# Turning the scan's sums once per block in four row groups, with the last products by C one unit earlier

## The chip, the cores and the metric

The kernel runs on one core of a Trainium2 chip. The metric is the device time of one execution in microseconds, from the first instruction to the last. A core has a matrix engine, TensorE (PE, with its weight loads listed as PEld), and three vector engines: VectorE (DVE), ScalarE (ACT) and GpSimd (POOL). SyncE (SP) issues the DMAs. Each engine works through its own queue in order, and a semaphore makes an instruction wait for one of another engine. Matmul results go to PSUM, which has eight banks of 512 fp32 columns on 128 partitions.

## What is computed

Two layers are applied to 16 images of 256 channels by 1024 tokens, each with a residual. The first is a transformer block. The second, which sets the order of the whole kernel, is a selective scan over the tokens, for 512 channels with 64 states each:

```
x = x + attention_and_mlp(group_norm(x))          # 4 heads of 32, LayerNorm, GELU
xs = group_norm(x) + pos
u, z = split(xs @ in_proj_w.T);  u = silu(causal_conv4(u))
dt, Bm, Cm = split(u @ x_proj_w.T)
delta = softplus(dt @ dt_proj_w.T + dt_proj_b);  A = -exp(A_log)
def step(h, (d_t, B_t, C_t, u_t)):                # h: 512 channels x 64 states
    h = exp(d_t[..., None] * A) * h + (d_t * u_t)[..., None] * B_t[:, None, :]
    y = einsum('bdn,bn->bd', h, C_t)
y = (ys + u * D) * silu(z);  x = x + (y @ out_proj_w.T) * sigmoid(conv3(xs))
```

The change concerns `y`: the sum over the 64 states of h times C, for each channel and each token.

## The kernel before, in words

**Units and blocks.** A unit is two channels: 2 x 64 states fill the 128 partitions, and 1024 tokens lie along the row. An image has 256 units. Eight units with slots i = 0 to 7 make a block of 16 channels, so an image has 32 blocks and the run has 4096 units in 512 blocks. The parity of a block is `e`. It says which of the two buffers `h0` and `h1` (128 x 8 x 1024) its scans fill.

**One unit** takes five instructions or so. `load` (L900) brings delta times u of its two channels from memory as `dub`, spread over the states (512 KB). `inputs` (L905) multiplies this by B on GpSimd. `decay` (L914) has two bf16 matmuls spread delta into the two banks of a tile `a`, and an exponential on ScalarE (L916) turns it into the decay. There are two `a` tiles, so the decay of unit n + 2 can start when the scan of unit n has read its tile. `scan` (L922) runs the recurrence on VectorE, 1024 steps in one instruction, into slot i of the block's buffer. `dub` has seven buffers; loads run six units ahead and multiplies four.

**The output of a block** (`outputs`, L939 to L979) is made while the next block is scanned. It has three stages, all in the one PSUM bank `yb`:
- *Products by C* (L955). The 1024 tokens are taken in 128 pieces of eight. For each piece a matmul with 32 columns of `cd`, which holds C on a diagonal, as weights and `h` at those eight tokens (64 columns of eight slots by eight tokens) as moving data writes 32 partitions. Each is an fp32 matmul, of which the profile shows two instructions. Two matmuls accumulate (c = 0, 1), and four in a row (g = 0 to 3) write the four groups of 32 partitions. Sixteen such sets of eight matmuls are numbered by r and s.
- *Copy* (L962). After the four sets of one r, ScalarE copies columns 0 to 255 of the bank to a tile `y2`. There are four copies per block.
- *Turns* (L945). Eight matmuls per r, with every eighth column of `y2` as weights and a constant `turn` as moving data (16 columns), put channels and tokens in an order in which they can be written to memory. They write 32 partitions, the same ones for all eight of an r, in columns 256 to 511. After the fourth r, ScalarE copies the result (64 x 256) to `yo` (L969), and eight DMAs (L977) of 8 KB each write it to `ys`.

**The order.** `outputs` is a generator. It hands control back at each `yield`, and the main loop takes one step of it per unit. In the loop a unit issues the load of unit n + 6, the multiply of n + 4, the scan of n, the decay of n + 2, then one or more steps of side work, and then one step of the running outputs. On each engine the program order is kept as it is recorded. A new block's `outputs` starts at its successor's slot 0, after the running one has had its step. The first eight steps have two sets of products each; the copy of r follows at the end of its second step, and its turns stand in the third step from its start, behind the next products. The fourth turn and the copy to `yo` are the ninth step, at slot 0 of the block after, and the DMAs are the twelfth.

Two waits follow from the buffers. The first scan of a block overwrites the `h` buffer of the block two before it, whose last products are the eighth step of that block's `outputs`, issued one unit earlier. And the first products of a block write the bank from which `yo` has just been copied.

**Side work** are the steps of attention and projections of the next image and of the gated output of the previous image. `rate_for` spreads them by their listed shares over the 256 units of an image. In the last image only the gated output of the one before is left.

The functions and lines that the steps below speak of:

Of the kernel before, what the change touches and what calls it, by code (L numbers as in the profile page):

```python
# [11 lines left out]
F32 = mybir.dt.float32  # L12
# [7 lines left out]
P = 128  # L20
# [30 lines left out]
def attention_then_scan_kernel(  # L51
# [18 lines left out]
    nc = tc.nc  # L70
    B = x.shape[0]

    def pool(name, bufs, **kw):
        return ctx.enter_context(tc.tile_pool(name=name, bufs=bufs, **kw))
# [8 lines left out]
    blk = pool("blk", 2)  # L83
    hst = pool("hst", 1)
# [77 lines left out]
    for k in range(ND):  # L162
# [4 lines left out]
        for j in range(2):  # L167
# [3 lines left out]
                start=(j == 0), stop=(j == 1),  # L171
# [3 lines left out]
    for e in range(2):  # L175
        some = ident[ds(64 * e, 48), ds(64 * e, 48)].rearrange("p (r j i) -> p r i j", r=3, j=2)
# [11 lines left out]
    turn = const.tile([P, 8, 2, 8], F32, name="turn")  # L188
# [27 lines left out]
    yb = yps.tile([P, HL], F32, name="yb", tag="yb")  # L216
# [721 lines left out]

    def outputs(b, k, q, e):  # L939
        hbuf = now["h", e]  # L940

        def turned(r, y2):
            some = yb[ds(32 * (r // 2), 32), 256:].rearrange("p (j a m x) -> p a x j m", j=2, a=2, m=8)
            for x in range(8):
                nc.tensor.matmul(  # L945
                    some[:, r % 2, x], y2[:, x : 256 : 8], turn[:, x], start=True, stop=True
                )

        y2 = None
        for r in range(4):  # L950
            for s in range(4):
                for c in range(2):
                    for g in range(4):
                        at = 256 * s + 64 * r + 16 * g + 8 * c
                        nc.tensor.matmul(  # L955
                            yb[ts(g, 32), ts(s, 64)],
                            cd[:, at // 16, ts(c, 32)], hbuf[:, :, at : at + 8],
                            start=(c == 0), stop=(c == 1),
                        )
                if s == 3:  # L960
                    y2 = blk.tile([P, 256], F32, name="y2", tag="y2")
                    nc.scalar.copy(y2, yb[:, :256])  # L962
                if s == 1 and r > 0:
                    turned(r - 1, y2)
                if s % 2 == 1:
                    yield
        turned(3, y2)
        yo = blk.tile([P, 256], F32, name="yo", tag="yo")
        nc.scalar.copy(yo[:64], yb[:64, 256:])  # L969
        for _ in range(3):  # L970
            yield
        to = state[b]["ys"][ds(k * P + 32 * q, 32)].rearrange(
            "(j i e) (s h c) -> e h s i j c", j=2, e=2, s=4, h=2
        )
        for h in range(2):
            for s in range(4):
                nc.sync.dma_start(  # L977
                    to[e, h, s], yo[ds(32 * h + 8 * s, 8)].rearrange("p (j c) -> p j c", j=2)
                )  # L979

    def prepare(b):
        return chain(first_norm(b), attention_layer(b), scan_inputs(b))
# [26 lines left out]
    for n, (b, k, q, e, i) in enumerate(units):  # L1009
        at = n % UNITS  # L1010
# [32 lines left out]
        if i == 0 and n > 0:  # L1043
            g = outputs(*units[n - 1][:4])
            next(g)
            running.append(g)
# [3 lines left out]
    for _ in outputs(*units[-1][:4]):  # L1050
        pass
# [71 lines left out]
```

## Time and profile before

| | |
|---|---|
| median of three runs | 15706.54 us (15690.69 to 15712.8) |
| the profiled execution, whole | 15708.14 us |
| its span, first to last instruction | 15706.0 us |
| mean granted TensorE clock | 0.725 of full speed |
| scans (L922), DVE | 4096, mean 2279 ns, 9238.5 us busy |
| multiplies (L905), POOL | 4096, mean 2391 ns, 9745.2 us busy |
| decay exponentials (L916), ACT | 4096, mean 1090 ns, 4464.5 us busy |
| copies to y2 (L962), ACT | 2048, mean 373 ns, 764.7 us busy |
| copies to yo (L969), ACT | 512, mean 365 ns, 187.0 us busy |

A row of groups gives the busy time of all instructions of one line and kind, the mean of one, and then the idle time of the engine just before them with what ended most of it. A row of waits names who waited for whom, the total, how often and the longest. In the timeline, equal neighbours are merged, and the brackets give the idle time ahead and its releaser. The view by windows gives for each stretch the busy time of each engine, the granted TensorE clock (1.00 is full), the share of DMA time, and GB/s. Busy time of PE is the union of its matmuls, of which several can run at once.

### The profile page before, as it was taken

The numbers are of one execution on the slowest core, as the hardware profiler recorded it, in microseconds if no ns is written. First come the engines' busy times: TensorE is split into PE (matmuls) and PEld (weight loads), VectorE is DVE, ScalarE is ACT, GpSimd is POOL, SyncE is SP. The second block draws the span as 40 slices with busy tenths as digits, with TensorE's granted clock in tenths as the row PEclk, the third lists the DMA queues.
The fourth block names the chain that finished last, engine by engine and source line by source line (L and its number), as shares of the span: only waits on it lengthen the run. The fifth ranks groups of instructions, "written<-read, shape, count | busy, mean of one in ns | idle before, by whom it ended". The sixth has DMA issues, their size and how long they took to land. (4 is left out here: it accounts for less than half of the span.)

```text
span 15706.0 us, 430046 instructions
## 1 busy us (share of the span) xinstructions
PE 12119.9 (77%) x186800; PEld 7304.2 (47%) x186800; DVE 11806.3 (75%) x7560; ACT 7635.3 (49%) x10421; POOL 9749.9 (62%) x4105
## 2 busy tenths in 40 slices
PE   7677877878778687787878878788787877878777
PEld 2344444444444444444444444444444444444455
DVE  3777787777877878778777787877877778677887
ACT  2455454545545545444554445545455454544544
POOL 0566666666666666566666666666666666666687
PEclk8776777767677676776767767677676877767756
DMA  1456455564555645556455565655556455564566
GB/s 53 168 172 206 159 185 188 174 204 158 190 177 173 205 161 192 174 174 203 162 191 181 171 200 166 197 172 176 196 172 203 163 181 195 167 206 161 183 220 203
DMA packets 989294, 2820.54 MB, mean 180 GB/s; under 512 B 175682, under 2 KB 319299, under 8 KB 987396
## 3 DMA queue, kind: packets, MB, share of 16 engines
q1 hardware_dynamic: 987396, 2793.03, 53.8%
q8 instruction: 1460, 23.92, 0.6%
q14 instruction: 438, 3.59, 0.1%
HBM read 2513.82 MB, written 261.62 MB: 177 GB/s over the span
## 5 line engine op out<-in xcount | busy, mean ns | idle before, releaser
L905 POOL TENSOR_TENSOR dub<-dub,bt 128x1024 f32<-128x1024 f32 x4096 | 9745.2, 2391 | 5895.1 <-DMA dub<-dus 5445.8
L922 DVE TENSOR_TENSOR_SCAN h<-a,dub 128x1024 f32<-128x1024 f32 x4096 | 9238.5, 2279 | 3031.0 <-ACT a L916 1458.8
L916 ACT ACTIVATE a<-a,acol 128x1024 f32<-128x1024 f32 x4096 | 4464.5, 1090 | 5315.2 <-PE a L914 5266.9
L914 PE MATMUL a<-pieces,pick 48*128 48x512 bf16 x8192 | 2054.2, 494 | 2669.0 <-DVE h L922 2578.7
L955 PEld LDWEIGHTS yb<-h,cd 128*32 128x32 f32 x131072 | 2713.8, 138 | 2812.5 <-issue 1522.2
L955 PE MATMUL yb<-h,cd 128*32 128x64 f32 x131072 | 3530.5, 266 | 549.1 <-ACT yo L969 334.2
L945 PEld LDWEIGHTS yb<-turn,y 128*32 128x32 f32 x32768 | 2222.6, 158 | 479.8 <-issue 269.5
L945 PE MATMUL yb<-turn,y 128*32 128x16 f32 x32768 | 2317.3, 216 | 32.5 <-ACT y L962 31.4
L914 PEld LDWEIGHTS <-pick 48*128 48x128 bf16 x8192 | 551.7, 96 | 3032.9 <-issue 2683.2
L962 ACT COPY y<-yb 128x256 f32<-128x256 f32 x2048 | 764.7, 373 | 1229.2 <-PE yb L955 1213.0
L435 PE MATMUL s_ps<-k,q 32*64 32x512 f32 x4092 | 851.6, 724 | 45.1 <-DVE mx L416 39.7
L491 PE MATMUL av<-pt,vv 128*64 128x512 f32 x2048 | 757.6, 828 | 2.2 <-ACT sums L480 1.6
L416 DVE TENSOR_REDUCE mx<-s_ps 128x1 f32<-128x512 f32 x1023 | 647.2, 676 | 110.6 <-PE s_ps L435 110.6
L503 PE MATMUL st_ps<-sp 33*128 33x512 f32 x2048 | 727.2, 794 | 2.9 <-ACT pt L511 2.9
L511 ACT ACTIVATE pt<-st_ps 128x512 f32<-128x512 f32 x1024 | 554.0, 595 | 186.7 <-PE st_ps L503 185.6
L688 PE MATMUL g_ps<-w,xp 128*128 128x256 f32 x1464 | 511.3, 495 | 0.0
L688 PEld LDWEIGHTS g_ps<-w,xp 128*128 128x128 f32 x1464 | 386.4, 327 | 89.9 <-issue 67.4
L969 ACT COPY yo<-yb 64x256 f32<-64x256 f32 x512 | 187.0, 365 | 481.6 <-PE yb L945 398.4
L674 DVE SCALAR_TENSOR_TENSOR u<-up,cwh,u 128x1024 f32<-128x1024 f32 x192 | 351.5, 1831 | 37.1 <-ACT u L666 36.9
L491 PEld LDWEIGHTS av<-pt,vv 128*64 128x64 f32 x2048 | 124.6, 165 | 512.2 <-issue 501.9
L435 PEld LDWEIGHTS s_ps<-k,q 32*64 32x64 f32 x4092 | 193.5, 148 | 343.0 <-DVE mx L416 248.1
L859 PE MATMUL m_ps<-w,xs 128*128 128x256 f32 x1024 | 335.9, 481 | 13.9 <-DVE xs L834 13.9
(177 smaller groups left out, 7029.1 us busy)
## 6 DMA issues: line engine op xcount, KB each, us to landing
dub<-dus SPq DMA_DIRECT2D x4096, 512.0 KB
ys<-yo SPq DMA_DIRECT2D x4096, 8.0 KB
dps<-pc SPq DMA_DIRECT2D x384, 128.0 KB
pieces<-dps SPq DMA_DIRECT2D x1024, 48.0 KB
xs<-in_x_dram SPq DMA_DIRECT2D x64, 512.0 KB
xs<-kept SPq DMA_DIRECT2D x64, 512.0 KB
zs<-z SPq DMA_DIRECT2D x64, 512.0 KB
ud<-u SPq DMA_DIRECT2D x64, 512.0 KB
```

The source lines that it names most:

```text
L416: nc.vector.tensor_reduce(mx[:, g, c, hf : hf + 1], s, AX.X, ALU.max)
L435: nc.tensor.matmul(waiting[g][0][ts(e, 64)], q4[r, ts(c, 64)], k4[r, hs(hf)], start=True, stop=True,)
L491: nc.tensor.matmul(av[ts(e, 2 * DH)], vv[j // (NJ // 2)][:, j % (NJ // 2), 2 * pair + e, :], pts[e], start=(j == 0), stop=(j == NJ - 1),)
L503: nc.tensor.matmul(s, ka[r, ts(j, P)], qa[r, hs(hf)], start=True, stop=True)
L688: nc.tensor.matmul(ps[:, ts(q, C)], xp[k][:, ds(first + t, P, 4)], wg_s[:, k, t, :], start=(k == 0 and t == 0), stop=False,)
L905: nc.gpsimd.tensor_tensor(v, v, blocks[units[n][0]]["bt"], ALU.mult)
L914: nc.tensor.matmul(a[:, hs(hf)], w, pieces[r], start=True, stop=True)
L916: nc.scalar.activation(a, a, AF.Exp, scale=acol[:, at : at + 1])
L922: nc.vector.tensor_tensor_scan(now["h", e][:, i, :], decays.pop(n), loaded.pop(n), 0.0, ALU.mult, ALU.add)
L945: nc.tensor.matmul(some[:, r % 2, x], y2[:, x : 256 : 8], turn[:, x], start=True, stop=True)
L955: nc.tensor.matmul(yb[ts(g, 32), ts(s, 64)], cd[:, at // 16, ts(c, 32)], hbuf[:, :, at : at + 8], start=(c == 0), stop=(c == 1),)
L962: nc.scalar.copy(y2, yb[:, :256])
```

## The change

The sums of a block are kept in one tile `y2` of 128 x 4 x 256, and all 32 turns are made in one step, after all products. For each of the eight x, four turns in a row write the four groups of 32 partitions. The pieces of eight tokens are dealt out by r and s the other way round. The products of one r go to one half of the bank, those of the next to the other half (`(r + e) % 2`), and the turns go to the first 128 columns of half `e`. The yields move: the seven steps with products have 3, 2, 2, 2, 2, 2 and 3 sets, the eighth step has the turns, the ninth the copy to `yo` (128 x 128 now), and the twelfth two DMAs of 32 KB in pieces of 64 tokens (256 bytes), where there were eight DMAs with pieces of 128 tokens.

```
     def outputs(b, k, q, e):
         hbuf = now["h", e]
-        def turned(r, y2):
-            some = yb[ds(32 * (r // 2), 32), 256:].rearrange("p (j a m x) -> p a x j m", j=2, a=2, m=8)
-            for x in range(8):
-                nc.tensor.matmul(
-                    some[:, r % 2, x], y2[:, x : 256 : 8], turn[:, x], start=True, stop=True
-                )
-        y2 = None
+        y2 = hst.tile([P, 4, 256], F32, name="y2", tag="y2")
         for r in range(4):
             for s in range(4):
                 for c in range(2):
                     for g in range(4):
-                        at = 256 * s + 64 * r + 16 * g + 8 * c
+                        at = 256 * r + 64 * s + 16 * g + 8 * c
                         nc.tensor.matmul(
-                            yb[ts(g, 32), ts(s, 64)],
+                            yb[ts(g, 32), ds(256 * ((r + e) % 2) + 64 * s, 64)],
...
-                if s == 3:
-                    y2 = blk.tile([P, 256], F32, name="y2", tag="y2")
-                    nc.scalar.copy(y2, yb[:, :256])
-                if s == 1 and r > 0:
-                    turned(r - 1, y2)
-                if s % 2 == 1:
+                if (r, s) in ((0, 2), (1, 0), (1, 2), (2, 0), (2, 2), (3, 0)):
                     yield
-        turned(3, y2)
-        yo = blk.tile([P, 256], F32, name="yo", tag="yo")
-        nc.scalar.copy(yo[:64], yb[:64, 256:])
+            nc.scalar.copy(y2[:, r], yb[:, ts((r + e) % 2, 256)])
+        yield
+        some = yb[:, ds(256 * e, P)].rearrange("p (j m x) -> p x j m", j=2, m=8)
+        for x in range(8):
+            for r in range(4):
+                nc.tensor.matmul(
+                    some[ts(r, 32), x], y2[:, r, x:256:8], turn[:, x], start=True, stop=True
+                )
+        yield
+        yo = blk.tile([P, P], F32, name="yo", tag="yo")
+        nc.scalar.copy(yo, yb[:, ds(256 * e, P)])
         for _ in range(3):
             yield
         to = state[b]["ys"][ds(k * P + 32 * q, 32)].rearrange(
-            "(j i e) (s h c) -> e h s i j c", j=2, e=2, s=4, h=2
+            "(j i e) (a c) -> e j a i c", j=2, e=2, a=16
         )
-        for h in range(2):
-            for s in range(4):
-                nc.sync.dma_start(
-                    to[e, h, s], yo[ds(32 * h + 8 * s, 8)].rearrange("p (j c) -> p j c", j=2)
-                )
+        for j in range(2):
+            nc.sync.dma_start(to[e, j], yo[:, ts(j, 64)])
```

The number of matmuls of each kind and their shapes stay: 128 products and 32 turns per block.

## The prediction, on record before the changed kernel was run

> **What bounds the kernel now.** I read the page's first part and its groups, then the list of waits, then the scan rows of the whole trace, then single blocks in the timeline, and last the busy times by stage.
>
> ```profile
> PE 12119.9 (77%) x186800; PEld 7304.2 (47%) x186800; DVE 11806.3 (75%) x7560; ACT 7635.3 (49%) x10421; POOL 9749.9 (62%) x4105
> ...
> L955 PE MATMUL yb<-h,cd 128*32 128x64 f32 x131072 | 3530.5, 266 | 549.1 <-ACT yo L969 334.2
> ...
> L945 PE MATMUL yb<-turn,y 128*32 128x16 f32 x32768 | 2317.3, 216 | 32.5 <-ACT y L962 31.4
> ```
>
> No engine is full; two are near it. A quarter as many instructions keep TensorE (PE) busy for two thirds as long in the turns (L945) as in the products by C (L955). Sixteen turn rows in one column group take 1.13 us (mean of 2047 bursts), 32 product rows over four groups 0.86 us (0.65 at full clock).
>
> ```profile
> DVE h L922 <- ACT a L916: 1458.8, 838, 8.4
> DVE h L922 <- PE yb L955: 1058.5, 310, 8.2
> ```
> ```profile
> PE a L914 <- DVE h L922: 2578.7, 1488, 11.3
> PE yb L955 <- ACT yo L969: 334.2, 511, 5.3
> PE yb L955 <- ACT y L962: 193.9, 320, 3.4
> ```
>
> These are VectorE's (DVE) and PE's waits (total, times, longest). Scans wait for products, and decay matmuls (L914) wait for scans: the two engines stop each other in turn. From the starts of the 4096 scans: in the second to fifteenth image, a block's eight scan-to-scan gaps are 2.82, 2.89, 4.72, 3.46, 3.78, 3.26, 3.11 and 6.24 us, of which DVE is busy 2.8 to 3.15. So the gap into the next block idles 3.41 us and the third gap 1.57, of some 7.2 per block. The timeline shows one boundary:
>
> ```profile
> 8597.54 0.65 PE L955 MATMUL yb<-h,cd 128*32 128x64 f32 x32
> 8601.05 0.61 PE L914 MATMUL a<-pieces,pick 48*128 48x512 bf16 x2 [2.86 <-DVE h L922]
> 8601.43 1.94 PE L503 MATMUL st_ps<-sp 33*128 33x512 f32 x4
> 8603.30 1.97 PE L491 MATMUL av<-pt,vv 128*64 128x512 f32 x4
> 8605.20 1.17 PE L945 MATMUL yb<-turn,y 128*32 128x16 f32 x16
> 8606.83 1.08 PE L955 MATMUL yb<-h,cd 128*32 128x64 f32 x32 [0.45 <-ACT yo L969]
> ```
> ```profile
> 8598.71 6.65 DVE L922 TENSOR_TENSOR_SCAN h<-a,dub 128x1024 f32<-128x1024 f32 x3 [3.96 <-PE yb L955]
> 8609.69 2.29 DVE L922 TENSOR_TENSOR_SCAN h<-a,dub 128x1024 f32<-128x1024 f32 x1 [4.32 <-ACT a L916]
> ```
>
> The old block's last products end at 8598.2. Only then may the first scan overwrite that buffer, after 3.96 us of DVE idleness, and only after this scan does the next decay run, after 2.86 us of PE idleness. Three scans pass; the fourth waits 4.32 us, because PE first did side work, turn, wait for yo, and products. PE's clock suffers too (us busy per engine, then granted clock):
>
> ```profile
> 8593.03:8596.44 3.41, 3.41 (x79) 1.72 (x79) 1.72 (x1) 2.64 (x5) 2.35 (x1) 1.00 0.69 190
> 8596.44:8599.86 3.42, 1.75 (x48) 1.43 (x48) 1.15 (x1) 1.39 (x2) 2.37 (x2) 1.00 0.40 151
> 8599.86:8603.27 3.41, 2.22 (x6) 0.67 (x5) 3.41 (x3) 1.09 (x1) 2.34 (x1) 0.50 0.16 64
> ```
>
> After a window with PE busy 1.75 of 3.42 us, the next is at half clock. Hence L503 takes 1.94 us there and 1.02 at full clock.
>
> The stages differ. Two of them, from the same view (scores; attention values):
>
> ```profile
> 8386.30:8478.20 91.90, 78.66 (x1200) 38.35 (x1199) 81.61 (x72) 31.60 (x39) 56.43 (x25) 0.83 0.41 145
> 8508.60:8712.10 203.50, 177.21 (x2588) 91.18 (x2591) 123.82 (x56) 113.40 (x170) 128.76 (x56) 0.74 0.50 160
> ```
>
> The first is three blocks bound by DVE (27.2 of 30.6 us each), the second seven bound by PE (25.3 of 29.1).
>
> **The change, part by part.** All prices are per block; there are 512.
>
> *The last products, a unit earlier.* Sums now stand 24, 16, 16, 16, 16, 16, 24 and 0 matmuls in the eight units; the eighth holds only turns. The old block's buffer is read out before the eighth scan has ended, so the boundary wait goes. On DVE it is worth between 2.07 us (1058.5 / 512, the named wait) and 3.41 (the gap's idle time, part of which the list puts down to ACT). Where PE binds, what goes is PE's own idleness behind that scan, 2.2 to 2.3 us in the gap after it. Late next is the exponential of the decay (ACT a).
>
> *Turns in four column groups.* 64 rows as before, but neighbours now write different groups of 32 partitions, as the products do. At the products' cadence (0.65 to 1.08 us for 32) they take 1.3 to 2.2 us in place of 4 x 1.13 = 4.52. Not overlapped at all they still take 4.5, in one unit. I take 1.3, nearest to L955: **-3.2 us of PE**. They no longer stand in the first unit ahead of the fourth scan's decay, which made the third gap.
>
> *Waits inside a step.* In the second, fourth and sixth unit the order is 8 products, copy, 8 products. The halves do not part them: the order of the changed program has the ninth product wait for the copy just issued. Before agrees: L955, writing columns 0 to 255, waited 511 times for yo, which reads columns 256 up. A copy takes 0.37 us. In before it began 0.12 us (median) or 0.46 (mean) after its products ended, and 0.05 passed until PE went on: 0.88 us, three times, 2.6. The bounds are 0.46 (ACT free) and 1.74 (L969's mean wait of 0.65 plus a whole exponential of 1.09). Gone are the old y waits, 193.9 / 512 = 0.4. Queued behind the wait are 8 products, then the decay of the next unit, then its exponential, then a scan. At a block's start the yo wait loses the turn that lay ahead of it, and meets the exponential: +0.3, between 0 and 1.1. Net **+2.5 us of PE**, so the turns' gain is nearly spent.
>
> *Copies and writes.* yo shrinks from 256 to 128 columns: from L969's 0.365 and 0.595 for 512 columns (L511) I estimate 0.26, so 0.1 us of ACT is saved, hidden (ACT is 49% busy). SP issues 2 DMAs for 8 (8 took 3.5 to 4.8 us), also hidden, since SP waits 7080 us for scans; without that cover it would gain 3 us. The pieces shrink to 256 bytes: packets of that size took 16.5 ns, of 512 bytes 30.5, so twice as many cost the same.
>
> **The sum.** DVE-bound stages: the scores blocks idle 3.46 us (1.88 at the boundary, 1.58 in the third gap); I leave 0.5, so -3.0. Mixed stages: boundary -3.4, PE otherwise -0.7 (turns less waits), against some 1.2 of gap that comes back as waits for ACT a: -2.9. PE-bound: -2.3 of idleness, -0.7, and half of what the half-clock window costs (L503 +0.92, L491 +0.89, L955 +0.43, L914 +0.22, sum 2.5): -1.3, together -4.3. Seven of 32 blocks at -4.3 and 25 at -2.9 are -3.2 on average; over 480 blocks -1540. The last image (21.7 us per block, 19.1 of it POOL's eight multiplies of 2.39) gains 2.3 x 32 = 74. 15708 - 1614 gives **14,100 us**. The profiled execution took 15708.1 us around a span of 15706.0, 1.6 above the median of the three runs. A measurement can tell about 0.2% from no change. With the bounds: a boundary of 2.07 and waits of 1.74 leave a gain near 0.1 us per block (15,650); both gaps wholly gone, 3.41 + 1.57 over 480 blocks and 2.28 + 0.68 over the last image's 32, give 2490 us (13,220).
>
> **The rivals.**
> - *The clock holds.* Without the boundary gap PE stays at full clock and PE-bound blocks near their DVE time: 24 us instead of 24.8, mixed ones lose 1.3 more. 13,500 us, chance 0.15. For it: a window 70 to 80% busy at full clock was followed by full clock 96 times in 100, and a wait of 0.9 us leaves 74%.
> - *Turns do not overlap, or waits are long.* A unit of 4.5 us of turns, or waits near 1.5 us, take back all but 1.2 us per block: 15,100 us, chance 0.17. For it: turns read y2 with a stride, and their weight load takes 158 ns against 110 (medians).
> - *The bubble only moves.* Every scan released at the boundary waits for ACT a instead: 15,700 us, within 0.2%, chance 0.05. Against it: the three scans after a boundary run with no gap.
> - *The clock falls: slower.* Four waits per block split PE's work. At full clock, windows 60 to 70% busy kept it 40 times in 100, those at 40 to 60% 23 times, and half clock ended only after windows over 80% busy, mostly over 95%. If two waits share a window (together over 1.4 us of 3.41), PE sinks to about 0.57, the clock of the stretch 9028 to 9143. Half clock then covers 0.86 of the time in place of 0.52; at 1.75 times the duration (1.94 / 1.02, 1.08 / 0.65, 0.61 / 0.39) PE's 22.1 us become 27.2, plus 4.3 idle (4.0 in before, less 2.3, plus 2.6): 31.5 against 29.1. Twenty of 32 blocks at +2.4 against twelve at -2.9 make +13 us per image: 15,900 us, chance 0.11.
>
> The Trainium skill's page "TensorE: Matmul & The Clock Gate" speaks for this last rival in its section "A second HAM failure mode: psum-queue depth-cycling": PE micro-idling between groups of matmuls that cycle through PSUM lets the clock swing. By that rule 15,900 would be the time. The same page's section "Why this matters for your kernels" warns only of idle gaps over about 3 us, which would leave the clock up. The trace lies between: a gap of 2.86 us lowered it.
>
> **How the numbers follow.** The forecast has 0.52 (its own range 13,700 to 14,600). The range 13,450 to 15,300 takes in the first two rivals and leaves out 0.2. Faster is 0.52 + 0.15 + 0.17 = 0.84, same 0.05, slower 0.11.
>
> **What would show it.** In the changed profile: no scan waiting for yb; turns busy near 700 us and not 2300; PE waiting for the y copy some 1500 times, 0.9 us each; PE's wait for scans at L914 shorter; granted clock at 0.725 or above; the eighth gap near 3 us. Turns at 2300, a clock under 0.65, or waits over 1.7 us would make it wrong.

## The result and the profile after

The changed kernel takes 14195.55 us (median of four runs, 14167.44 to 14220.53) beside 15709.67 us for the kernel before: a ratio of 0.9038, with a 95% interval of 0.9019 to 0.9057. That is 1514 us less. The forecast was 14,100 us.

The first lines are from the page of the changed kernel (its profiled execution: a span of 14201.1 us, mean granted clock 0.774). The products are now L947, the copies to y2 L954, the turns L959 and the copies to yo L964.

```profile
PE 10371.0 (73%) x186800; PEld 5556.7 (39%) x186800; DVE 11797.6 (83%) x7560; ACT 7533.6 (53%) x10421; POOL 9760.8 (69%) x4105
...
L947 PE MATMUL yb<-h,cd 128*32 128x64 f32 x131072 | 3626.0, 260 | 2318.4 <-ACT y L954 1687.0
...
L959 PE MATMUL yb<-turn,y 128*32 128x16 f32 x32768 | 611.9, 217 | 124.5 <-ACT y L954 124.3
```

VectorE (DVE) does the same work in less time: 83% of the span, not 75%. The turns, 32768 rows as before, occupy TensorE (PE) for 612 us in place of 2317. But the products, which used to idle 549 us before them, now idle 2318. The lists of waits of DVE and of PE say on whom:

```profile
DVE h L922 <- ACT a L916: 972.3, 833, 8.5
DVE h L922 <- PE yb L947: 472.6, 258, 7.0
```
```profile
PE yb L947 <- ACT y L954: 1687.0, 1536, 6.1
PE a L914 <- DVE h L922: 1016.7, 994, 10.0
PE yb L947 <- ACT yo L964: 612.6, 377, 6.3
```

Scans wait 473 us for products, not 1059, and decays 1017 us for scans, not 2579. On the other side stands a wait that was 194 us before: 1687 us for the copies to y2, 1536 times, exactly three per block.

The same two stretches as before, three blocks of scores and seven of attention values, by the view of windows (busy times, then granted clock):

```profile
7593.50:7674.50 81.00, 67.70 (x1202) 28.20 (x1200) 81.00 (x74) 31.12 (x40) 56.39 (x25) 1.00 0.46 165
7700.00:7880.70 180.70, 150.59 (x2624) 68.71 (x2623) 125.93 (x56) 113.79 (x173) 131.88 (x57) 0.81 0.55 184
```

In the scores stretch DVE is busy 81.00 of 81.00 us: nothing is left to gain there but DVE's own work. The clock is 1.00 and was 0.83. The attention stretch fell from 29.1 to 25.8 us per block, with PE busy 83% of it. A part of the timeline of PE in the scores stretch shows a block boundary and a wait inside a step; its last two lines are from a boundary in the attention stretch, the stage of the boundary shown in the prediction:

```profile
7594.59 1.20 PE L959 MATMUL yb<-turn,y 128*32 128x16 f32 x64
7595.78 0.39 PE L914 MATMUL a<-pieces,pick 48*128 48x512 bf16 x2
7596.36 1.67 PE L435 MATMUL s_ps<-k,q 32*64 32x512 f32 x8 [0.19 <-DVE mx L416]
7597.97 0.88 PE L947 MATMUL yb<-h,cd 128*32 128x64 f32 x48
7599.16 0.39 PE L914 MATMUL a<-pieces,pick 48*128 48x512 bf16 x2 [0.31 <-DVE h L922]
7599.74 1.67 PE L435 MATMUL s_ps<-k,q 32*64 32x512 f32 x8 [0.19 <-DVE mx L416]
7601.34 0.43 PE L947 MATMUL yb<-h,cd 128*32 128x64 f32 x16
7602.32 0.43 PE L947 MATMUL yb<-h,cd 128*32 128x64 f32 x16 [0.55 <-ACT y L954]
...
7725.35 1.19 PE L959 MATMUL yb<-turn,y 128*32 128x16 f32 x64 [0.17 <-ACT y L954]
7727.37 0.39 PE L914 MATMUL a<-pieces,pick 48*128 48x512 bf16 x2 [0.83 <-DVE h L922]
```

In the scores stretch the turns of one block and the products of the next stand only a decay and side work apart, with waits of at most 0.19 us between them. At the attention boundary PE's wait for the scan is 0.83 us, where it was 2.86. The 64 turn rows take 1.20 us. At 7602.32 the second half of a step has waited 0.55 us for a copy of 0.37.

From the scan starts of the second to fifteenth image, the eight gaps are now 2.91, 3.05, 3.75, 3.39, 3.48, 3.32, 3.06 and 4.20 us. The gap into the next block idles 1.39 us and not 3.41, the third 0.65 and not 1.57.

### The profile page after: what moved, and what is told of

Same layout as the page of the kernel before. It is cut to its first block, busy times and chain, and to the rows that moved or that the text cites. A ratio compares the mean times of both kernels' runs of the same rounds, so it can differ in the third digit from the quotient of the medians.

```text
span 14201.1 us, 424620 instructions
## 1 busy us (share of the span) xinstructions
PE 10371.0 (73%) x186800; PEld 5556.7 (39%) x186800; DVE 11797.6 (83%) x7560; ACT 7533.6 (53%) x10421; POOL 9760.8 (69%) x4105
## 4 chain that ended last, share of the span: by engine, by line
PE 39%; DVE 27%; ACT 14%; issue 12%; DMA 6%; POOL 1%; SPq 1%; DVEq 0%; ACTq 0%; POOLq 0%
DVE h L922 17%; PE yb L947 11%; PE a L914 6%; ACT a L916 5%; DVE mx L416 4%; PE av L491 4%; PE st_ps L503 3%; DMA dub<-dus 3%; ACT y L954 2%; PE m_ps L859 2%; PE g_ps L688 2%; PE z_ps L639 2%; POOL dub L905 1%; PE u_ps L660 1%; PE yb L959 1%
## 5 line engine op out<-in xcount | busy, mean ns | idle before, releaser
L905 POOL TENSOR_TENSOR dub<-dub,bt 128x1024 f32<-128x1024 f32 x4096 | 9756.0, 2395 | 4388.0 <-DMA dub<-dus 4071.5
L922 DVE TENSOR_TENSOR_SCAN h<-a,dub 128x1024 f32<-128x1024 f32 x4096 | 9246.8, 2280 | 1591.0 <-ACT a L916 972.3
L947 PE MATMUL yb<-h,cd 128*32 128x64 f32 x131072 | 3626.0, 260 | 2318.4 <-ACT y L954 1687.0
L947 PEld LDWEIGHTS yb<-h,cd 128*32 128x32 f32 x131072 | 2630.4, 132 | 4735.1 <-ACT y L954 1984.8
L914 PE MATMUL a<-pieces,pick 48*128 48x512 bf16 x8192 | 1956.8, 471 | 1054.1 <-DVE h L922 1016.7
L954 ACT COPY y<-yb 128x256 f32<-128x256 f32 x2048 | 765.6, 374 | 1039.8 <-PE yb L947 1032.0
L914 PEld LDWEIGHTS <-pick 48*128 48x128 bf16 x8192 | 507.6, 96 | 1500.8 <-issue 1207.1
L959 PEld LDWEIGHTS yb<-turn,y 128*32 128x32 f32 x32768 | 561.0, 159 | 414.9 <-ACT y L954 221.6
L959 PE MATMUL yb<-turn,y 128*32 128x16 f32 x32768 | 611.9, 217 | 124.5 <-ACT y L954 124.3
L491 PE MATMUL av<-pt,vv 128*64 128x512 f32 x2048 | 695.3, 764 | 2.7 <-ACT sums L480 1.6
L503 PE MATMUL st_ps<-sp 33*128 33x512 f32 x2048 | 658.1, 725 | 2.4 <-ACT pt L511 2.4
L688 PE MATMUL g_ps<-w,xp 128*128 128x256 f32 x1464 | 453.2, 449 | 0.0
L491 PEld LDWEIGHTS av<-pt,vv 128*64 128x64 f32 x2048 | 118.0, 156 | 466.3 <-issue 456.3
L859 PEld LDWEIGHTS m_ps<-w,xs 128*128 128x128 f32 x1024 | 262.5, 328 | 54.7 <-issue 32.3
```

What stands on the lines that cost most here:

```text
L491: nc.tensor.matmul(av[ts(e, 2 * DH)], vv[j // (NJ // 2)][:, j % (NJ // 2), 2 * pair + e, :], pts[e], start=(j == 0), stop=(j == NJ - 1),)
L503: nc.tensor.matmul(s, ka[r, ts(j, P)], qa[r, hs(hf)], start=True, stop=True)
L688: nc.tensor.matmul(ps[:, ts(q, C)], xp[k][:, ds(first + t, P, 4)], wg_s[:, k, t, :], start=(k == 0 and t == 0), stop=False,)
L905: nc.gpsimd.tensor_tensor(v, v, blocks[units[n][0]]["bt"], ALU.mult)
L914: nc.tensor.matmul(a[:, hs(hf)], w, pieces[r], start=True, stop=True)
L922: nc.vector.tensor_tensor_scan(now["h", e][:, i, :], decays.pop(n), loaded.pop(n), 0.0, ALU.mult, ALU.add)
```

## Experiments

Theory A, from the prediction: the boundary coming off the chain is the gain, while the shorter turns only pay for the new waits. Its rival, theory B: PE's shorter turns are the gain. Each run stands beside runs of the kernel before on its own chip (medians of 15,669 to 15,726 us), and the differences are against those. Where the edit names no other base, it is on the changed kernel.

| run | time, us | against before | ratio (95%) |
|---|---|---|---|
| the change | 14195.55 | -1514 | 0.904 (0.902 to 0.906) |
| schedule only | 15285.06 | -441 | 0.971 (0.968 to 0.974) |
| turns only | 14719.90 | -1006 | 0.935 (0.932 to 0.938) |
| boundary alone | 14225.82 | -1468 | 0.907 (0.904 to 0.909) |
| steps end at copies | 13452.26 | -2274 | 0.855 (0.852 to 0.859) |
| yo with turns | 13808.22 | -1918 | 0.878 (0.875 to 0.880) |
| both waits out | 13142.91 | -2551 | 0.838 (0.836 to 0.839) |
| heavy step last | 13223.68 | -2470 | 0.843 (0.842 to 0.845) |
| few turns | 13136.54 | -2532 | 0.838 (0.837 to 0.840) |
| one half | 14197.71 | -1471 | 0.907 (0.905 to 0.908) |
| eight DMAs | 14366.19 | -1328 | 0.915 (0.913 to 0.917) |

**Schedule only**, on the kernel before:

```
-                if s % 2 == 1:
+                if (r, s) in ((0, 2), (1, 0), (1, 2), (2, 0), (2, 2), (3, 0)):
                     yield
+        yield
         turned(3, y2)
+        yield
```

> The kernel before with only the yields moved: products done in seven steps (3, 2, 2, 2, 2, 2, 3 sets), turns still four times per block in one column group, yo and its eight DMAs as before. Theory A (the gain is the boundary wait off the chain; in the changed kernel the shorter turns, 3.3 us of PE per block, only pay for the new waits inside steps, 1.1 us each): here the waits come and nothing pays for them, PE +2.9 us per block, so blocks bound by VectorE gain some 2 us and blocks bound by PE lose some 0.6: 15,300 us (14,900 to 15,600). Theory B (the gain is PE's shorter turns, and the boundary wait shrinks only because PE has less to do): no gain, 15,700 us or above, with scans still waiting about 1000 us for yb.

Measured 15,285 us, as A says. The waits inside steps came in full (PE for the y copy 1642.7 us, 1536 times). Yet one sign that B named is there. DVE's list:

```profile
DVE h L922 <- ACT a L916: 1327.2, 1094, 8.5
DVE h L922 <- PE yb L955: 1030.2, 383, 8.6
```

Moving the last products a unit ahead does not by itself end the wait for them: PE falls behind by more than a unit. The cause is mainly the waits inside steps and not the long turns, since *boundary alone*, below, has the same long turns without these waits, and its scans wait 238.3 us. What shrank here is the idle time of the gap, from 3.41 to 2.38 us.

**Turns only**: the products back in eight steps of two sets.

```
-                if (r, s) in ((0, 2), (1, 0), (1, 2), (2, 0), (2, 2), (3, 0)):
+                if s == 1:
                     yield
             nc.scalar.copy(y2[:, r], yb[:, ts((r + e) % 2, 256)])
-        yield
+            yield
...
-        yield
         yo = blk.tile([P, P], F32, name="yo", tag="yo")
```

> The changed kernel with the products back in eight steps of two sets, each copy at the end of a step; the 32 turns in four groups stand in the ninth step with the copy to yo. Theory A: the boundary wait stays (near 1000 us named, gap into the next block near 5.5 us), the third gap closes and PE saves 3.3 us per block with no waits inside steps: 14,900 us (14,600 to 15,200). Theory B: nearly the whole gain of the change, 14,200 to 14,400 us.

Measured 14,720 us. B is refuted as the whole, but by itself this part is worth 1006 us: two thirds of the change (some 170 of them from the six DMAs fewer, if these are worth here what the run with eight DMAs shows for the change). The gap into the next block is 5.44 us, as A says; the scans' wait for yb, 775.2 us, is less than the 1000 it named. That the third gap would close was wrong: it still idles 1.30 us; turns and yo stand in the first unit here.

**Boundary alone**, on the kernel before: old turns, old DMAs, no wait inside a step.

```
-                if s % 2 == 1:
+                if s == 3 or (r > 0 and s == 1):
                     yield
         turned(3, y2)
+        yield
```

> The kernel before with its old turns (one column group, four times a block) and old DMAs, and 4, 2, 2, 2, 2, 2, 2 sets, so that the products end a unit earlier and no copy is waited for inside a step: the boundary alone. Theory A (the boundary is worth what the schedule alone gained, 441 us, plus what the waits inside steps cost, 743): 14,550 us (14,300 to 14,800). Rival (with the long turns PE is too late for the boundary to open at all, and the schedule's gain is mostly the third gap): 15,000 to 15,300 us.

Measured 14,226 us, 74 us below A's range and 324 below its sum of 441 and 743. With four sets in the first step, each copy ends its step. The lists of DVE and PE:

```profile
DVE h L922 <- PE yb L955: 238.3, 140, 7.0
```
```profile
PE a L914 <- DVE h L922: 1468.6, 1161, 11.5
PE yb L955 <- ACT y L962: 190.4, 219, 5.5
```

This order with no waits bought is worth 1468 us, nearly as much as the whole change (1514). It is not the boundary alone in the strict sense: the fourth turn also leaves the first unit of the next block. By the scan starts of the second to fifteenth image, a block idles 2.95 us less than before, 2.30 of them in the gap into the next block and 0.59 in the third gap. No run parts the two. *Steps end at copies*, the next run, adds the shorter turns and the fewer DMAs to this order and is 774 us faster; the waits inside steps, by the same run, cost the change 743. So in the change these two nearly cancel.

The stages part the two theories further. By the same scan starts, a scores block takes 30.7 us before and in *turns only*, and 27.0 here, in the change and in *steps end at copies*: there the order gives the whole gain and the turns nothing. An attention block takes 29.4 us before, 25.2 in *turns only*, 24.5 here, 25.4 in the change and 21.7 in *steps end at copies*: where PE binds, either part alone gives about what the change gives, and both together without the waits give almost twice as much.

**Steps end at copies**: the waits inside steps taken out of the change.

```
-                if (r, s) in ((0, 2), (1, 0), (1, 2), (2, 0), (2, 2), (3, 0)):
+                if r > 0 and s == 1:
                     yield
             nc.scalar.copy(y2[:, r], yb[:, ts((r + e) % 2, 256)])
-        yield
+            yield
```

> The changed kernel with 4, 2, 2, 2, 2, 2 and 2 sets in the seven steps, so that every copy to y2 is the last of its step and no product waits behind it inside a step. Theory A (the waits inside steps eat the turns' gain): PE's wait for the y copy falls from 1687 us to about 300, blocks bound by PE and mixed ones win 1.5 to 3 us, scores blocks (already bound by VectorE alone) nothing: 13,600 us (13,300 to 13,900). Rival (those waits lie in time that PE would have idled in any case, waiting for scans at the decay): 14,100 to 14,200 us, and PE's wait for scans at L914 grows by what the y waits lose.

Measured 13,452 us, 743 us less than the change. PE's list:

```profile
PE a L914 <- DVE h L922: 2212.2, 1888, 12.3
PE yb L947 <- ACT yo L964: 613.0, 393, 6.3
PE yb L959 <- ACT y L954: 135.1, 106, 5.0
PE yb L947 <- ACT y L954: 132.8, 205, 5.2
```

Of 1687 us of waiting for y, 133 are left. The rival had a point: 1196 us came back as waits for scans. But the time still fell by half of what was freed. Scans wait 174.7 us for yb, no longer 472.6: PE's lateness, made by these waits, had kept most of that wait alive.

**yo with turns**: the copy to yo in the eighth step.

```
                 )
-        yield
         yo = blk.tile([P, P], F32, name="yo", tag="yo")
         nc.scalar.copy(yo, yb[:, ds(256 * e, P)])
+        yield
```

> The changed kernel with the copy to yo at the end of the eighth step, right behind the turns, and not in the ninth behind the next unit's exponential. Theory A (every wait of PE on a copy costs where PE binds): the first products of a block wait near 0.2 us in place of 1.2 (612.6 us in all), 0.5 to 0.9 us per block come back: 13,900 us (13,750 to 14,100). Rival (ScalarE, held by the copy until the turns end, starts the next exponential late, and the scan waits for that): 14,200 to 14,400 us, with more wait of scans for ACT a.

Measured 13,808 us, 387 less than the change. The lists of PE and DVE:

```profile
PE yb L947 <- ACT yo L963: 62.7, 48, 2.0
```
```profile
DVE h L922 <- ACT a L916: 725.9, 679, 7.8
```

PE's wait for yo fell from 612.6 us to 62.7 (48 times), and scans waited for ACT a 725.9 us and not 972.3: the rival, a late exponential, did not come.

**Both waits out**: the two edits above together.

> The changed kernel with both earlier moves at once: 4, 2, 2, 2, 2, 2, 2 sets, every copy to y2 at the end of its step, and the copy to yo right behind the turns. Theory A (each wait of PE on a copy costs by itself, 743 and 387 us in the two single runs): close to the sum, 13,050 to 13,250 us. Rival (what is left is VectorE's own work and the first of the two moves has already reached it): 13,350 to 13,450 us.

Measured 13,143 us. The sum of the single gains would be 13,066, so they are nearly independent. It is the fastest version that computes all of y, 0.838 of the kernel before (0.836 to 0.839) and 1053 us ahead of the change. Its stretches of scores and attention values:

```profile
7009.50:7090.60 81.10, 66.56 (x1204) 28.59 (x1200) 81.10 (x74) 31.43 (x40) 58.09 (x26) 1.00 0.47 165
7115.90:7265.40 149.50, 132.70 (x2622) 63.87 (x2621) 124.68 (x56) 112.79 (x173) 129.37 (x57) 0.91 0.65 219
```

The scores blocks had nothing left to win. Seven attention blocks take 149.5 us in place of 180.7, and the clock is 0.91.

**Heavy step last**, on the fastest version: `if r < 3 and s == 1:` in place of `if r > 0 and s == 1:`, so the sets are 2, 2, 2, 2, 2, 2, 4.

> As the run before it, with the step of four sets last and not first: 2, 2, 2, 2, 2, 2, 4 sets, then the turns. Theory A (what counts on PE is how late the decay behind each step comes): the third gap, which the first step makes, shrinks, and the four sets stand where the gap into the next block may open; equal to the run before or better by up to 100 us. Rival (products that end late in the seventh unit bring the scans' wait for yb back): 100 to 300 us slower than the run before, with the wait of scans for yb above 300 us.

Measured 13,224 us, 81 slower than with the heavy step first, near the rival: scans wait 404.7 us for yb and not 152.7. Here slack before the boundary was worth more than slack behind it.

**Few turns**, on the fastest version: `for x in range(1)` in place of `range(8)`, which leaves out 28 of a block's 32 turns and so seven eighths of y.

> The fastest kernel so far (4, 2, 2, 2, 2, 2, 2 sets, yo copied behind the turns) with 4 of the 32 turns of each block; the other 28 are left out, so seven eighths of y are not computed. This takes another 1 us of PE work per block (some 500 us in all) away. If VectorE's own work is now the bound: 13,143 less 100 at most. If PE's work still sets the pace as in the change itself, where 3.3 us per block were worth 2 us: 12,800 to 12,900 us.

Measured 13,137 us, the same. PE's work is no longer the price: its wait for scans grew from 2373 to 2580 us and its clock fell from 0.798 to 0.773. Beside the boundary, shorter turns and fewer DMAs were worth 774 us; on the fastest version, less PE work is worth nothing more.

**One half**: the halves undone.

```
-                            yb[ts(g, 32), ds(256 * ((r + e) % 2) + 64 * s, 64)],
+                            yb[ts(g, 32), ts(s, 64)],
...
-            nc.scalar.copy(y2[:, r], yb[:, ts((r + e) % 2, 256)])
+            nc.scalar.copy(y2[:, r], yb[:, :256])
...
-        some = yb[:, ds(256 * e, P)].rearrange("p (j m x) -> p x j m", j=2, m=8)
+        some = yb[:, ds(256, P)].rearrange("p (j m x) -> p x j m", j=2, m=8)
...
-        nc.scalar.copy(yo, yb[:, ds(256 * e, P)])
+        nc.scalar.copy(yo, yb[:, ds(256, P)])
```

> The changed kernel with all products in columns 0 to 255 and all turns in columns 256 to 383, for every r and both parities: the halves undone. If the whole bank is the unit of waiting, nothing changes: 14,195 us within 40, and PE waits for the y copy 1536 times, near 1690 us. If the halves do part products from copies, the waits lengthen and the time goes to 14,400 us or above.

Measured 14,198 us with 1536 waits for y of 1689.9 us in all: no difference clear of noise. The halves of the bank do nothing, because in this program products wait for a copy of any columns of it. The Trainium skill's page "PSUM — Partial Sum Buffer", section "PSUM bank collisions raise a hardware error", gives the reason to keep them apart by bank and group of 32 partitions and not by column. No run here let them meet.

**Eight DMAs**: the layout of the change, but eight issues per block.

```
-            "(j i e) (a c) -> e j a i c", j=2, e=2, a=16
+            "(j i e) (r a c) -> e j r a i c", j=2, e=2, r=4, a=4
         )
         for j in range(2):
-            nc.sync.dma_start(to[e, j], yo[:, ts(j, 64)])
+            for r in range(4):
+                nc.sync.dma_start(to[e, j, r], yo[ts(r, 32), ts(j, 64)])
```

> The changed kernel with each block's ys written by eight DMAs of 8 KB as in the kernel before, in the same pieces of 256 bytes. Theory A (SP's time lies under its waits for scans): no change, 14,195 us within 40. Rival (the six further issues, 0.5 us each, delay the loads of dub): 14,300 us or above, with POOL waiting longer for dub.

Measured 14,366 us, some 170 more than the change: the rival. Most of it is not spread out: by the scan starts of this run and of the change, three gaps per image (in the second block, in the eighteenth, and into the next image) are each 2.8 to 2.9 us longer, 8.6 of the 13.7 us that an image takes longer (second to fifteenth image). POOL's wait for dub, which the rival named, grew by 31 us only (4071.5 to 4102.5): at the place shown below it is another load that comes late. The timeline of SP and of DVE in the second block of an image, in the run with eight DMAs:

```profile
7524.74 0.64 SPq L343 DMA_DIRECT2D xs<-ys  x1
7525.48 5.12 SPq L972 DMA_DIRECT2D ys<-yo  x8
7530.70 0.56 SPq L900 DMA_DIRECT2D dub<-dus  x1
7531.31 0.59 SPq L343 DMA_DIRECT2D xs<-ud  x1
```
```profile
7536.74 2.11 DVE L830 SCALAR_TENSOR_TENSOR xs<-xs,vec 128x1024 f32<-128x1024 f32 x1 [8.65 <-DMA xs<-ud]
```

and in the change:

```profile
7462.73 0.64 SPq L343 DMA_DIRECT2D xs<-ys  x1
7463.46 1.21 SPq L971 DMA_DIRECT2D ys<-yo  x2
7464.77 0.56 SPq L900 DMA_DIRECT2D dub<-dus  x1
7465.38 0.58 SPq L343 DMA_DIRECT2D xs<-ud  x1
```
```profile
7471.31 2.12 DVE L830 SCALAR_TENSOR_TENSOR xs<-xs,vec 128x1024 f32<-128x1024 f32 x1 [5.23 <-DMA xs<-ud]
```

Eight issues hold SP 5.1 us, and the load that DVE needs next stands behind them in the same queue: DVE idles 8.65 us and not 5.23.

## Why the prediction was right, step by step

- **The boundary: right in kind, too clean.** "The boundary wait goes" was said of the scan's wait for yb. It fell from 1059 to 473 us, and the gap's idleness from 3.41 to 1.39 us. The eighth gap is 4.20 us and not near 3. What failed is the thought that one unit of lead suffices. Where PE is late by more than a unit the wait stays, and *steps end at copies* shows that the new waits make most of that lateness (472.6 to 174.7 us). In *boundary alone* the gap into the next block idles 2.30 us less, inside the bounds of 2.07 and 3.41; the run's 1468 us (2.87 per block) hold more than that gap, as said there.
- **The turns: right.** 1.20 us per burst, 1.3 forecast: -3.3 us of PE per block.
- **The waits inside steps: right in kind, low in size.** 1687.0 / 1536 = 1.10 us each, 0.88 forecast; the yo wait 612.6 / 512 = 1.20 per block, 0.95 forecast. Less the old ones, they cost PE (1687 - 194 + 613 - 334) / 512 = 3.46 us, 2.5 forecast. What was too small is the delay: in the trace of the change the three copies inside steps begin 0.67 us (mean) after their products end, where 0.46 was taken from before; with 0.37 for the copy and 0.05 until PE goes on that is 1.09. Turns less waits are +0.1 us, not -0.7.
- **Copies and writes: wrong for SP.** The prediction called SP's saved issues hidden, "since SP waits 7080 us for scans", with 3 us per block if that cover went. The cover goes at three places per image, which make about two thirds of some 170 us. A queue that idles on average can still be in the way at the few places where a needed load stands behind a burst of issues. The 256-byte packets, forecast at 16.5 ns, took 18.2 in the change (mean of 132,096), so twice as many cost a little more and not the same.
- **The clock: right in direction.** It rose from 0.725 to 0.774, 0.74 to 0.81 in the attention stretch and 0.83 to 1.00 in the scores. L503's mean fell from 794 to 725 ns and L491's from 828 to 764. How much of the time this made cannot be parted from the rest: no run held the clock alone.
- **The sum.** -3.2 us per block were forecast, and over 15 images a block lost 3.05 (an image went from 967 us to 869, mean of 15); the last image lost 37 us and not 74. By stage: scores 30.7 to 27.0 (-3.0 forecast), attention values 29.4 to 25.4 (-4.3 forecast). The mixed stages, all put at -2.9, came to -2.7 in the mean of 22 blocks, but ranged from -0.6 (blocks 18 to 20, where the copies were late already, 1.29 us in before) to -5.7 (24 to 26): their mean was near, one figure for all was not. Block 20 even grew, from 31.8 to 36.1 us. That the sum came out so close is partly luck: the 0.7 us that turns less waits were to give did not come, and the third gap, not priced in the mixed stages, gave 0.9 us less idle time.
- **The rivals.** "Turns do not overlap" fell with 1.20 us. "The clock falls" fell too, for the whole: the mean clock rose, and windows 60 to 70% busy at full clock kept it 84 times in 100 in the change (40 in before). Single blocks did sink: block 20 from 0.79 to 0.67 (mean of images 2 to 15). That rival's arithmetic was also a little off: 203.50 less 177.21 over seven blocks is 3.8 us of idle time per block, not 4.0, which takes some 60 us off its 15,900. The Trainium skill's rule on the clock and PSUM cycling (the page and section named in the prediction) did not show in the scores stretch: waits of about half a microsecond come three times a block and the clock stays at 1.00. In the attention stretch it is not ruled out: the clock is 0.81 with the waits and 0.91 in *both waits out*. "The clock holds" put 13,500 us on the change. *Steps end at copies* is 13,452, but at a mean clock of 0.792, so the two times meet without that rival's full clock being shown.

## What to carry to other kernels

A buffer that is read to the end of one period and overwritten at the start of the next can lock two engines to each other, though neither is full (77% and 75% busy here); look for the pair of waits that name each other, and finish the reading a step earlier. When an output is moved inside a pipelined step, put each copy where other work of the waiting engine follows, since a wait behind a copy in the middle of a step is paid for in good part (743 us of 1554 here, 387 of 550 for the copy at the block's start). Ask of every queue what stands behind a burst, and not only how long it idles.

## What was not expected of the hardware

- Columns of one bank do not part engines in this program: 14,196 us with halves and 14,198 with one half.
- Less work on PE lowered its clock with no loss of time: 28 turns fewer per block took the granted clock from 0.798 to 0.773, at 13,143 and 13,137 us. So a lower clock was no sign of a loss there, where PE waits for scans.
- One issue of the writes to `ys` on SP took 0.59 us (median) for 32 KB in the change and 0.58 us for 8 KB in the run with eight DMAs, so two DMAs beat eight DMAs of the same bytes and pieces by 170 us. In the kernel before, whose pieces are of 512 bytes, one issue of 8 KB took 0.30 us; why, no run shows.
